# Weighted sums of an attention kernel on four column tiles of 32 channels by 128 rows, two tiles of keys at a time

## The chip, the cores and the metric

The kernel runs on one core of one Trainium2 chip. The metric is device time in microseconds (us), from the start of the program to its end, without the host. Two runs of the kernel before gave 1893.37 and 1893.46 us, a median of 1893.41. The profile is one execution of the same program taken by the hardware profiler.

The engines of a core work side by side and wait for one another by semaphores: PE (TensorE, matrix multiplication into PSUM), DVE (VectorE), ACT (ScalarE), POOL (GpSimd) and SP (SyncE, which only issues transfers). The profile shows PE's matmuls and its weight loads (PEld) apart.

## The reference

The input is a batch of 8 images of 64 channels and 64 x 64 pixels (4096 pixels per image). Layer 0 is attention over the pixels of an image, layer 1 three binarized convolutions with a gate. Cut to what matters:

```python
q, k, v = wq @ x + bq, wk @ x + bk, wv @ x + bv           # each 64 x 4096 per image
q, k = q - mean(q), k - mean(k)
sim = softmax(q.T @ k / 8, axis=keys)                      # 4096 x 4096 per image
out = sim @ v + out_unary                                  # out_unary: one vector per image
x = x + out
# layer 1: three convolutions (1x1, 3x3, 5x5) of sign(x) with sign weights, scaled and summed
s = conv1(sign(x)) + conv3(sign(x)) + conv5(sign(x))
result = s * sigmoid(gate(mean(s))) + x
```

## The kernel before, in words

**Tiles.** Two images make a pair; image 0 takes partitions 0 to 63, image 1 partitions 64 to 127 (one partition per channel). There are 4 pairs. The 4096 queries of a pair are cut into 8 blocks of 512 columns, so the whole kernel runs 32 blocks one after the other. Within a block, the 4096 keys of an image are cut into 32 tiles of 128 keys. All matrices of the attention are 32-bit floats.

**One step of a block** handles one tile of keys for both images:

- `scores` (L573): four matmuls of 64 rows (channels) by 64 columns (half of the keys, `h`), for two halves and two images `b`, over 512 queries. The result `ps`, 128 keys x 2 images x 512 queries, lies in two PSUM banks. The pool `ps_s` holds two such results, and other stages borrow from it.
- ACT takes the exponential (L595) of `ps` into `e` in SBUF. The pool `ep` holds five such tiles; the partial sums of the softmax of the block before (`e_parts`, L652) borrow one of the five from step 0 to step 7.
- `weighted` (L598): four matmuls (L607) of 64 rows (half of the keys) by 64 columns (channels of one image). Half `h` accumulates into bank `acc[h]`, over all 32 tiles of keys. So each bank has the sum over half of the keys, for both images.
- `summed` (L615): DVE adds `e` to `es` (L625; L623 for the first two), the sums of the softmax. Tiles 5, 11, 17 and 23 are added in DRAM instead, by a DMA of POOL's queue (L644, L646).

**The loop** (`attend`, L1217) keeps the weighted sum one tile behind: in each step it issues the scores of tile j, then the weighted sum and the adding of tile j - 1, then what the plan has put at this step. `pending` carries the tile that is still to be summed, also from one block to the next. On PE, scores and weighted sums so take turns.

**The plan** (`plan`, L1227) is a list of further work by step number. In step 0, after the last weighted sum of the block before: `weighted_out` (L627) copies `acc[0]` by ACT (L632) and `acc[1]` by DVE (L633) to SBUF; `send` and `gather` move the partial sums through DRAM; `mix_rows` (L1125) computes the queries of a coming block (`pq`, L563) and the convolution's row products of the block three back (L906, L996), for which it borrows one `ps_s` tile (`banks5`) and both `acc` banks. DVE and ACT read these products with L937, L939 and L944. Steps 5 to 7 fold the partial sums on DVE (`fold_first` L661, `fold` L666 and L667, `fold_last` L671). Step 13 adds the two halves of the weighted sum (`added`, L717), step 15 divides and adds the input (`finish`, L721 and L722), steps 16 to 20 take signs. In the last four blocks of a pair, steps 14 and 22 compute value tiles of the next pair (`values`, `pv` L414), which also borrow a `ps_s` tile; ACT copies them (L422) and takes an exponential (L429). Steps 18 to 24 prepare the convolution's row combinations on DVE. Four times in the run `unary_end` (`po`, L461) multiplies on the whole 128 x 128 array.

**The last block** cuts its queries into two parts (`PARTS`, L43): 384 columns with 32 steps, and 128 columns with 8 steps of four tiles of keys each. Its plan (`plan_last`, L1346) puts the work of the step by this number of steps, and adds two calls of `mix` (L1072) for the convolution, which borrow from `ps_s`.

The order on each engine follows the program's order of issue (`manual_schedule`), apart from what the recording layer interleaves between engines; a buffer's next user waits for its last user.

Of the kernel before, what the change touches and what calls it, by code (L numbers as in the profile page):

```python
# [18 lines left out]
F32 = mybir.dt.float32  # L19
# [3 lines left out]
ALU = mybir.AluOpType  # L23
# [3 lines left out]
P = 128  # L27
# [4 lines left out]
QB = 512  # L32
NQ = N // QB
NK = N // P
# [8 lines left out]
PARTS = ((slice(0, 384), 1), (slice(384, QB), 4))  # L43
# [4 lines left out]
def conv_seq_kernel(ctx, tc, x, wqv, wk, wv, w1, w3, w5, wtap, gw, out):  # L48
    nc = tc.nc
# [3 lines left out]
    img = [slice(0, C), slice(C, P)]  # L53
# [5 lines left out]
    fp = ctx.enter_context(tc.tile_pool(name="fp", bufs=1))  # L59
# [219 lines left out]
    class Pair:  # L279
# [3 lines left out]
        def __init__(self, name, xt):  # L283
            self.name, self.x = name, xt
            self.xs = sm.tile([P, 8], F32, tag="xs", name=f"xs_{name}")
            self.q, self.x2, self.s, self.y1, self.acc, self.o = {}, {}, {}, {}, {}, {}
            self.sides = []
            self.es, self.r, self.joint, self.sc, self.gap, self.t = {}, {}, None, None, None, None

# [308 lines left out]
        def weighted(self, qb, j, e, part=(slice(0, QB), 1)):  # L598
            cols, n = part
            w = cols.stop - cols.start  # L600
            if j == 0:
                self.acc[qb] = acc_banks(f"acc_{self.name}_{qb}_{cols.start}")
            for t in range(n * j, n * j + n):
                at = (t - n * j) * w
                for b in range(2):
                    for h in range(2):
                        nc.tensor.matmul(  # L607
                            self.acc[qb][h][img[b], 0:w],
                            self.v[img[h], t, img[b]],
                            e[img[h], b, at : at + w],  # L610
                            start=(t == 0),
                            stop=(t == NK - 1),
                        )

        def summed(self, qb, j, e, dram=False, begin=nc.vector):  # L615

# [10 lines left out]
        def weighted_out(self, qb, cols=slice(0, QB)):  # L627

            acc, w = self.acc.pop(qb), cols.stop - cols.start
            if cols.start == 0:  # L630
                self.o[qb] = [self.tile(fp, f"o{h}", qb) for h in range(2)]
            nc.scalar.copy(self.o[qb][0][:, cols], acc[0][:, 0:w])  # L632
            nc.vector.tensor_copy(self.o[qb][1][:, cols], acc[1][:, 0:w])  # L633

# [68 lines left out]
        def reciprocals_wide(self, qb, cols):  # L705
            if cols.start == 0:
                self.r[qb] = self.tile(fp, "r", qb)
            for a in range(cols.start, cols.stop, P):
                c = slice(a, min(a + P, cols.stop))
                sums, at = self.sums_p  # L710
                nc.vector.reciprocal(self.r[qb][:, c], sums[:, c.start - at : c.stop - at])

        def added(self, qb, cols=slice(0, QB)):
            if cols.start == 0:
                self.x2[qb] = self.tile(bp, "x2", qb)
            o = self.o[qb]
            nc.vector.tensor_tensor(self.x2[qb][:, cols], o[0][:, cols], o[1][:, cols], ALU.add)  # L717

        def finish(self, qb, cols=slice(0, QB)):
            x2 = self.x2[qb][:, cols]  # L720
# [486 lines left out]
    def acc_banks(name):  # L1207
        return [ps_a.tile([P, QB], F32, tag=f"acc{h}", name=f"{name}_{h}") for h in range(2)]

    def misc_banks(name):  # L1210
        return [m_tile(f"{name}_{h}") for h in range(2)]

# [2 lines left out]
        return slice(pr * P, (pr + 1) * P)  # L1215

    def attend(pairs, early):  # L1217
        pending = None
        n_blocks = n_pairs * NQ

        def block(g):
# [5 lines left out]
        def plan(g):  # L1227
# [4 lines left out]
            def put(i, f, *a):  # L1232
                at.setdefault(i, []).append((f, a))
# [36 lines left out]
            if g >= 1:  # L1270
                put(5, p.fold_first, b)
                put(6, p.fold, b)
                put(7, p.fold_last, b)
                put(8, p.spread, b)
                put(9, p.check_block, b, 0)
                put(11, p.check_block, b, 1)
                at0 = 13 if g < n_blocks - 1 else 11
                put(at0, p.added, b)
                put(at0 + 2, p.finish, b)
                put(at0 + (3 if g < n_blocks - 1 else 4), p.signs_wide, b, 2)  # L1280
                put(at0 + (5 if g < n_blocks - 1 else 6), p.signs_wide, b, 1)
                put(at0 + 7, p.signs, b)
# [63 lines left out]
        def plan_last():  # L1346

            at, (first, _) = {}, PARTS
            for i, steps in plan(n_blocks - 1).items():
                at[i * QB // first[0].stop] = steps  # L1350

            def put(i, f, *a):
                at.setdefault(i, []).append((f, a))

            p, b = pairs[-1], NQ - 1
            cols = first[0]
            r1 = cols.stop // HH
            put(NK - 5, lambda: mix(None, rows(n_blocks - 3), one_bank, score_banks))
            put(NK - 2, lambda: mix(None, (p, p.joint_rows(0, 6)), one_bank, score_banks))
            put(NK, p.weighted_out, b, cols)  # L1360
            put(NK + 1, p.added, b, cols)
            put(NK + 1, p.sums_wide, b, first)
            put(NK + 1, p.reciprocals_wide, b, cols)
            put(NK + 2, p.finish, b, cols)
            put(NK + 3, lambda: p.check(p.r[b][:, cols], n_blocks - 1))
            put(NK + 4, p.signs_wide, b, 2, 0, r1)
            put(NK + 5, p.signs_wide, b, 1, 0, r1)
            put(NK + 6, p.signs, b, 0, r1)
            return at

        for g in range(n_blocks):
            pr, qb = divmod(g, NQ)
            last = g == n_blocks - 1
            at = plan_last() if last else plan(g)
            p = pairs[pr]
            parts = PARTS if last else ((slice(0, QB), 1),)
            steps = [(part, j) for part in parts for j in range(NK // part[1])]
            for i, (part, j) in enumerate(steps):
                first = g == 0 and j < len(early)
                e = early[j] if first else p.scores(qb, j, None, part)  # L1380
                new = (p, (qb, j, e), part)
                if pending is not None:
                    pending[0].weighted(*pending[1], pending[2])

                    begin = nc.gpsimd if pending[2] == PARTS[1] else nc.vector
                    pending[0].summed(*pending[1], g < n_blocks - 1, begin)
                for f, a in at.pop(i, ()):
                    f(*a)
                pending = new
            assert not at, at.keys()  # L1390
        pending[0].weighted(*pending[1], pending[2])
        pending[0].summed(*pending[1])


        p, b = pairs[-1], NQ - 1
# [2 lines left out]
        r0, r1 = cols.start // HH, ROWS  # L1398
        p.weighted_out(b, cols)
        p.sums_wide(b, part)  # L1400
        p.added(b, cols)
        p.reciprocals_wide(b, cols)
        p.check(p.r[b][:, cols], n_pairs * (NQ + 1), (0,))
        p.finish(b, cols)
# [1 line left out]
            p.signs_wide(b, n, r0, r1, None)  # L1406
            p.copy_signs(b, n, r0, r1, (nc.vector.tensor_copy, nc.gpsimd.tensor_copy))
        p.signs(b, r0, r1, nc.gpsimd.tensor_copy)

        def acc_bank(h):  # L1410
            return lambda name: [ps_a.tile([P, QB], F32, tag=f"acc{h}", name=name)]

        def count(side):
            p.check(p.r[b][:, cols], n_pairs * (NQ + 1), (side,))
# [69 lines left out]
    with tc.If(n_good < P):  # L1484
        neg = fp.tile([P, QB], F32, tag="t5", name="neg")
        nc.vector.memset(neg, 0.0)
        with tc.For_i(0, n_pairs * P, P) as row:
# [12 lines left out]
            for qb in range(NQ):  # L1500
                mix((p, qb), None)
                for h in range(QB // P):
                    part = sm.tile([P, 2, NQ], F32, tag="part", name=f"part_{qb}_{h}")
                    for kb_ in range(NQ):
                        ps = ps_s.tile([P, 2, QB], F32, tag="s", name=f"px_{qb}_{h}_{kb_}")
                        for b in range(2):
                            nc.tensor.matmul(
                                ps[:, b, :],
                                p.q[qb][img[b], bass.ts(h, P)],
                                p.x[img[b], bass.ts(kb_, QB)],  # L1510
                                start=True,
                                stop=True,
                            )
                        nc.vector.tensor_reduce(part[:, :, kb_], ps, AX.X, ALU.max)
                    nm = sm.tile([P, 2], F32, tag="nmx", name=f"nmx_{qb}_{h}")
                    nc.vector.tensor_reduce(nm, part, AX.X, ALU.max, negate=True)
                    pn = m_tile(f"pn_{qb}_{h}")
                    for b in range(2):
                        nc.tensor.matmul(
                            pn[C * b : C * b + 1, 0:P], nm[:, b : b + 1], ident, start=True, stop=True  # L1520
                        )
                        nc.vector.tensor_copy(
                            neg[C * b : C * b + 1, bass.ts(h, P)], pn[C * b : C * b + 1, 0:P]
                        )
                for j in range(NK):
                    e = p.scores(qb, j, neg)
                    p.weighted(qb, j, e)
                    p.summed(qb, j, e)
                p.weighted_out(qb)
                p.sums_wide(qb)  # L1530
                p.reciprocals_wide(qb, slice(0, QB))
                p.added(qb)
                p.finish(qb)
            p.copy_tile()
            for qb in range(NQ):
# [66 lines left out]
```

## Time and profile before

| what | value |
|---|---|
| median of two runs | 1893.41 us |
| span of the profiled execution, first to last instruction | 1889.9 us |
| granted TensorE clock, mean | 0.999 of full speed |
| PE busy with matmuls | 1875.6 us (99%) |
| PE weight loads | 800.7 us (42%), beside matmuls |
| DVE busy | 1602.8 us (85%) |
| ACT busy | 1269.5 us (67%) |
| POOL busy | 131.2 us (7%) |
| DMA, mean over the span | 75 GB/s |

How to read it: a group of instructions is a line of the kernel, its engine and operation, the result and the inputs by the program's names, its shape and count, then busy time in us, mean ns of one instruction, and the time for which the engine stood idle just before it with what ended that. A shape such as `64*64 64x512` is the part of the array (rows * columns), then partitions x elements of the streamed operand. Matmuls are pipelined and their ends are modelled, so starts say more than ends. A matmul on 32-bit floats leaves two records. The chain that ended last is followed back from the last instruction, at each step to what released it.

### The profile page before, as it was taken

The page shows a single profiled execution, that of the slowest core. Times are in us where ns is not written, and L with a number is a line of the kernel's source. Part 1 is how long each engine was busy: PE and PEld are TensorE (multiplying, and loading weights), DVE is VectorE, ACT ScalarE, POOL GpSimd, SP SyncE. Part 2 cuts the span into 40 slices and gives each one's busy share as a digit, 9 for nine tenths or more (in the row PEclk, how much of TensorE's full clock was granted, in tenths as well). Part 3 has the DMA queues.
Part 4 walks back from the last instruction along what each step waited for, and adds up shares of the span by engine and source line. Part 5 has one row for each costly group of instructions (what it writes and reads, how often), then busy time and mean ns, then how long its engine had stood idle before and what let it go on. Part 6 is the DMA issues. An engine that isn't in the chain of part 4 may idle for free.

```text
span 1889.9 us, 51407 instructions
## 1 busy us (share of the span) xinstructions
PE 1875.6 (99%) x22016; PEld 800.7 (42%) x22016; DVE 1602.8 (85%) x2526; ACT 1269.5 (67%) x1630; POOL 131.2 (7%) x176
## 2 busy tenths in 40 slices
PE   9999999999999999999999999999999999999997
PEld 4345344443344434443434444434433344444345
DVE  7888888889888888888888888888888888888886
ACT  6666776666666676666666667666666666666664
POOL 0000000000000000000000000000000000000001
PEclk9999999999999999999999999999999999999999
DMA  4334333333333433333333444243333333333311
GB/s 125 65 65 103 78 67 71 67 58 72 68 70 89 117 82 81 65 73 66 58 72 68 97 111 89 58 83 66 72 67 58 71 78 90 86 71 65 82 36 53
DMA packets 73461, 142.50 MB, mean 75 GB/s; under 512 B 10444, under 2 KB 41480, under 8 KB 73096
## 3 DMA queue, kind: packets, MB, share of 16 engines
q0 software_dynamic: 22320, 81.27, 23.3%
q1 hardware_dynamic: 50328, 56.73, 10.3%
q8 instruction: 174, 2.85, 0.6%
q10 hardware_dynamic: 576, 1.13, 0.2%
q14 instruction: 63, 0.52, 0.1%
HBM read 39.27 MB, written 89.78 MB: 68 GB/s over the span
## 4 chain that ended last, share of the span: by engine, by line
PE 98%; DVE 1%; ACT 0%; DMA 0%; issue 0%; ACTq 0%; DVEq 0%
PE ps L582 46%; PE acc L607 46%; PE z L906 2%; PE pv L414 1%; PE z L996 1%; PE pq L563 1%; DMA es<-e 0%; PE z_5e L906 0%; ACT e L595 0%; PE warm L157 0%; DVE es L625 0%; DVE sb L1069 0%; PE pq L535 0%; PE su L696 0%; DVE es_j L1028 0%
## 5 line engine op out<-in xcount | busy, mean ns | idle before, releaser
L595 ACT ACTIVATE e<-ps 128x1024 f32<-128x1024 f32 (+1 forms) x1030 | 1048.4, 1018 | 568.2 <-PE ps L582 553.0
L625 DVE TENSOR_TENSOR es<-es,e 128x1024 f32<-128x1024 f32 (+1 forms) x842 | 1019.7, 1211 | 192.5 <-ACT e L595 178.2
L582 PE MATMUL ps<-q,x 64*64 64x512 f32 (+2 forms) x8448 | 1090.3, 577 | 1.5 <-DVE q L347 0.8
L607 PE MATMUL acc<-e,v 64*64 64x512 f32 (+2 forms) x8432 | 1085.8, 576 | 1.3 <-ACT e L595 1.3
L607 PEld LDWEIGHTS acc<-e,v 64*64 64x64 f32 x8432 | 335.0, 131 | 545.8 <-ACT e L595 314.8
L582 PEld LDWEIGHTS ps<-q,x 64*64 64x64 f32 x8448 | 359.5, 133 | 483.3 <-issue 262.3
L646 POOL DMA_DIRECT2D es<-e x93 | 80.1, 861 | 903.8 <-ACT e L595 598.7
L976 DVE SCALAR_TENSOR_TENSOR sb<-pt,sb 128x256 f32<-128x256 f32 x174 | 65.8, 418 | 0.0
L906 PEld LDWEIGHTS <-wc 64*64 64x64 bf16 x3364 | 58.8, 106 | 1.7 <-issue 0.8
L646 POOL DMA_DIRECT2D es<-es x31 | 26.6, 857 | 438.6 <-DVE es L625 438.6
L623 DVE TENSOR_TENSOR es<-e,e 128x1024 f32<-128x1024 f32 (+1 forms) x31 | 37.7, 1216 | 17.2 <-ACT e L595 17.2
L906 PE MATMUL z<-ec,wc 64*64 64x128 bf16 x1392 | 51.5, 217 | 0.0
L906 PE MATMUL z<-t,wc 64*64 64x128 bf16 x1392 | 51.1, 216 | 0.1
L754 ACT ACTIVATE s<-x,wqv_s 128x512 bf16<-128x512 f32 (+2 forms) x66 | 46.2, 702 | 0.2 <-DVE x L722 0.2
L939 ACT ACTIVATE pt<-z,frac 128x256 f32<-128x256 f32 (+1 forms) x58 | 30.6, 578 | 16.8 <-PE z L906 16.8
L644 POOL DMA_DIRECT2D es<-e x31 | 17.5, 563 | 334.5 <-ACT e L595 323.3
L633 DVE COPY o<-acc 128x512 f32<-128x512 f32 (+2 forms) x33 | 22.3, 675 | 9.4 <-PE acc L607 9.3
L950 DVE TENSOR_TENSOR pt<-pt 128x384 f32<-128x384 f32 x58 | 29.6, 552 | 0.0
L414 PEld LDWEIGHTS pv<-wx,x 64*64 64x64 f32 x992 | 21.5, 134 | 16.1 <-issue 8.6
L661 DVE TENSOR_TENSOR e_parts<-e_parts 128x512 f32<-128x512 f32 x31 | 21.3, 686 | 6.1 <-DMA e_parts<-es 6.0
L722 DVE SCALAR_TENSOR_TENSOR x<-x,ou,x 128x512 f32<-128x512 f32 (+2 forms) x33 | 24.3, 736 | 1.2
L422 ACT COPY v<-pv 128x512 f32<-128x512 f32 x31 | 18.2, 587 | 8.4 <-PE pv L414 8.4
(201 smaller groups left out, 893.9 us busy)
## 6 DMA issues: line engine op xcount, KB each, us to landing
es<-e POOLq DMA_DIRECT2D x124, 512.0 KB, 5.1
es<-es POOLq DMA_DIRECT2D x31, 512.0 KB, 5.3
e_parts<-es SPq DMA_DIRECT2D x124, 128.0 KB, 3.0
r<-rc SPq DMA_DIRECT2D x62, 128.0 KB, 2.8
out<-sb SPq DMA_DIRECT2D x27, 256.0 KB, 2.9
x<-in_x SPq DMA_DIRECT2D x24, 256.0 KB, 4.3
ec<-t SPq DMA_DIRECT2D x29, 99.0 KB, 4.5
xc<-in_x SPq DMA_DIRECT2D x30, 72.0 KB
```

Of the source, the lines that this page charges most:

```text
L414: nc.tensor.matmul(pv[img[h], b, i * w : (i + 1) * w], self.x[img[b], bass.ds((4 * g + i) * P + h * H, H)], self.wx[img[b], 0:w], start=Tr ...
L582: nc.tensor.matmul(ps[img[h], b, i * w : (i + 1) * w], self.x[img[b], bass.ds((n * j + i) * P + h * H, H)], self.q[qb][img[b], cols], star ...
L595: nc.scalar.activation(e, ps[:, :, 0 : n * w], AF.Exp, scale=1.0 / 8.0)
L607: nc.tensor.matmul(self.acc[qb][h][img[b], 0:w], self.v[img[h], t, img[b]], e[img[h], b, at : at + w], start=(t == 0), stop=(t == NK - 1),)
L623: begin.tensor_tensor(self.es[qb], self.first, e, ALU.add)
L625: nc.vector.tensor_tensor(self.es[qb], self.es[qb], e, ALU.add)
L646: nc.gpsimd.dma_start(out=out, in_=e, accum_op=ALU.add)
L754: nc.scalar.activation(sy[n][0][:, rows, pad : pad + HH], self.x2[qb][:, r0 * HH : r1 * HH].rearrange("p (h w) -> p h w", w=HH), AF.Sign, ...
L906: nc.tensor.matmul(z[img[b], :].rearrange("p (q w) -> p q w", w=HH), wc[k][img[h], n, c * C : c * C + C], src[:, first : first + step + 1 ...
L939: nc.scalar.activation(out, z, AF.Identity, scale=frac[:, by : by + 1])
L950: nc.vector.tensor_tensor(self.pairs[:, :, :, r, :], t[:, 0:3, 0], t[:, 0:3, 1], op)
L976: nc.vector.scalar_tensor_tensor(out, x, by, out, ALU.mult, ALU.add, **gap)
```

## The change

1. `weighted` now issues four matmuls with all 128 rows (all keys of the tile) and 32 columns (half of the channels of one image) each; group `g` takes image `g // 2`. All four write one bank, each its own 32 partitions. One accumulator holds the whole sum.
2. With one accumulator, `weighted_out` is one ACT copy straight into `x2`; the DVE copy and the later addition (`added`) go, with all calls.
3. The loop takes two steps at a time: the scores of tiles i and i + 1, then the weighted sums and addings of the two tiles before, then what the plan has at steps i and i + 1.

```diff
@@ weighted
-                self.acc[qb] = acc_banks(f"acc_{self.name}_{qb}_{cols.start}")
+                self.acc[qb] = acc_bank(0)(f"acc_{self.name}_{qb}_{cols.start}")[0]
             for t in range(n * j, n * j + n):
                 at = (t - n * j) * w
-                for b in range(2):
-                    for h in range(2):
-                        nc.tensor.matmul(
-                            self.acc[qb][h][img[b], 0:w],
-                            self.v[img[h], t, img[b]],
-                            e[img[h], b, at : at + w],
-                            start=(t == 0),
-                            stop=(t == NK - 1),
-                        )
+                for g in range(4):
+                    nc.tensor.matmul(
+                        self.acc[qb][32 * g : 32 * g + 32, 0:w],
+                        self.v[:, t, 32 * g : 32 * g + 32],
+                        e[:, g // 2, at : at + w],
+                        start=(t == 0),
+                        stop=(t == NK - 1),
+                    )
@@ weighted_out
             if cols.start == 0:
-                self.o[qb] = [self.tile(fp, f"o{h}", qb) for h in range(2)]
-            nc.scalar.copy(self.o[qb][0][:, cols], acc[0][:, 0:w])
-            nc.vector.tensor_copy(self.o[qb][1][:, cols], acc[1][:, 0:w])
+                self.x2[qb] = self.tile(bp, "x2", qb)
+            nc.scalar.copy(self.x2[qb][:, cols], acc[:, 0:w])
@@ added: removed, with its calls in the plans, at the end and in the fallback path
-        def added(self, qb, cols=slice(0, QB)):
-            if cols.start == 0:
-                self.x2[qb] = self.tile(bp, "x2", qb)
-            o = self.o[qb]
-            nc.vector.tensor_tensor(self.x2[qb][:, cols], o[0][:, cols], o[1][:, cols], ALU.add)
@@ moved up, from the end of attend
+    def acc_bank(h):
+        return lambda name: [ps_a.tile([P, QB], F32, tag=f"acc{h}", name=name)]
@@ attend
-        pending = None
+        pending = []
...
-            for i, (part, j) in enumerate(steps):
-                first = g == 0 and j < len(early)
-                e = early[j] if first else p.scores(qb, j, None, part)
-                new = (p, (qb, j, e), part)
-                if pending is not None:
-                    pending[0].weighted(*pending[1], pending[2])
-
-                    begin = nc.gpsimd if pending[2] == PARTS[1] else nc.vector
-                    pending[0].summed(*pending[1], g < n_blocks - 1, begin)
-                for f, a in at.pop(i, ()):
-                    f(*a)
+            for i in range(0, len(steps), 2):
+                new = []
+                for part, j in steps[i : i + 2]:
+                    first = g == 0 and j < len(early)
+                    e = early[j] if first else p.scores(qb, j, None, part)
+                    new.append((p, (qb, j, e), part))
+                for old in pending:
+                    old[0].weighted(*old[1], old[2])
+                    begin = nc.gpsimd if old[2] == PARTS[1] else nc.vector
+                    old[0].summed(*old[1], g < n_blocks - 1, begin)
+                for k in (i, i + 1):
+                    for f, a in at.pop(k, ()):
+                        f(*a)
                 pending = new
             assert not at, at.keys()
-        pending[0].weighted(*pending[1], pending[2])
-        pending[0].summed(*pending[1])
+        for old in pending:
+            old[0].weighted(*old[1], old[2])
+            old[0].summed(*old[1])
```

More of the change, by code (lines that the diff above doesn't have):

```diff
@@ L285, in __init__ @@
             self.xs = sm.tile([P, 8], F32, tag="xs", name=f"xs_{name}")
-            self.q, self.x2, self.s, self.y1, self.acc, self.o = {}, {}, {}, {}, {}, {}
+            self.q, self.x2, self.s, self.y1, self.acc = {}, {}, {}, {}, {}
             self.sides = []
@@ L1277, in plan @@
                 at0 = 13 if g < n_blocks - 1 else 11
-                put(at0, p.added, b)
                 put(at0 + 2, p.finish, b)
@@ L1360, in plan_last @@
             put(NK, p.weighted_out, b, cols)
-            put(NK + 1, p.added, b, cols)
             put(NK + 1, p.sums_wide, b, first)
@@ L1400, in attend @@
         p.sums_wide(b, part)
-        p.added(b, cols)
         p.reciprocals_wide(b, cols)
@@ L1408, in attend @@
         p.signs(b, r0, r1, nc.gpsimd.tensor_copy)
-        def acc_bank(h):
-            return lambda name: [ps_a.tile([P, QB], F32, tag=f"acc{h}", name=name)]
         def count(side):
@@ L1531, in conv_seq_kernel @@
                 p.reciprocals_wide(qb, slice(0, QB))
-                p.added(qb)
                 p.finish(qb)
```

## The prediction

> **What bounds the kernel now.** I read the shares of the engines first, then the chain that ended last, then the costliest groups.
>
> ```profile
> PE 1875.6 (99%) x22016; PEld 800.7 (42%) x22016; DVE 1602.8 (85%) x2526; ACT 1269.5 (67%) x1630; POOL 131.2 (7%) x176
> ...
> PE 98%; DVE 1%; ACT 0%; DMA 0%; issue 0%; ACTq 0%; DVEq 0%
> PE ps L582 46%; PE acc L607 46%; PE z L906 2%; PE pv L414 1%; PE z L996 1%; PE pq L563 1%; DMA es<-e 0%; PE z_5e L906 0%; ACT e L595 0%; PE warm L157 0%; DVE es L625 0%; DVE sb L1069 0%; PE pq L535 0%; PE su L696 0%; DVE es_j L1028 0%
> ...
> L595 ACT ACTIVATE e<-ps 128x1024 f32<-128x1024 f32 (+1 forms) x1030 | 1048.4, 1018 | 568.2 <-PE ps L582 553.0
> L582 PE MATMUL ps<-q,x 64*64 64x512 f32 (+2 forms) x8448 | 1090.3, 577 | 1.5 <-DVE q L347 0.8
> L607 PE MATMUL acc<-e,v 64*64 64x512 f32 (+2 forms) x8432 | 1085.8, 576 | 1.3 <-ACT e L595 1.3
> ```
>
> TensorE is 98% of the chain, and scores (L582) and weighted sums (L607) idle 1.5 and 1.3 us in all. Whatever lengthens TensorE lengthens the kernel. The timeline of TensorE in a steady stretch gives its beat:
>
> ```profile
> 1003.33 1.06 PE L607 MATMUL acc<-e,v 64*64 64x512 f32 x8
> 1004.19 1.06 PE L582 MATMUL ps<-q,x 64*64 64x512 f32 x8
> 1005.05 1.06 PE L607 MATMUL acc<-e,v 64*64 64x512 f32 x8
> ```
>
> A group starts every 0.86 us: four matmuls, two records each, so two passes of 0.43 us in which four 64x64 tiles stream together. Of the 1.06, 0.43 is the first pass and 0.59 one record (L607's mean by shape is 589 ns); the remaining 0.04 is the stagger of the four starts.
>
> **How the array changes shape.** Only `po` (L461), on 128x128, stands between such groups, four times. The timeline around the last of them, matmuls, then weight loads:
>
> ```profile
> 1404.88 1.06 PE L607 MATMUL acc<-e,v 64*64 64x512 f32 x8
> 1405.87 0.49 PE L461 MATMUL po<-vu,ones 128*128 128x130 f32 x2
> 1406.29 1.09 PE L582 MATMUL ps<-q,x 64*64 64x512 f32 x8
> 1407.20 0.61 PE L607 MATMUL acc<-e,v 64*64 64x512 f32 x4
> ```
> ```profile
> 1404.88 0.17 PEld L607 LDWEIGHTS acc<-e,v 64*64 64x64 f32 x4
> 1405.87 0.30 PEld L461 LDWEIGHTS po<-vu,ones 128*128 128x128 f32 x2 [0.81 <-DVE pt L944]
> 1406.29 0.21 PEld L582 LDWEIGHTS ps<-q,x 64*64 64x64 f32 x8
> ```
>
> The load for `po` begins 0.99 us after the group, not 0.86: 0.13 late, of which 0.04 is the stagger, 0.09 an empty array. The following scores take 0.91 instead of 0.86: their weights couldn't be loaded ahead, 0.05. After a switch the stagger is 0.02 (the next groups last 1.04).
>
> **The Trainium skill.** *TensorEngine Tiling (Array Packing)*, Key Properties, says that changing the tiling mode, not just the tile, drains TensorE; the 0.09 agrees. *TensorE: Matmul & The Clock Gate*, LDWEIGHTS, gives columns/1.2 ns: 53 for 64 columns, as the trace has, 27 for 32. The same page, "What overlaps and what doesn't", has loads overlap matmuls only where row groups differ, which would spoil tiles of 128 rows. The trace disagrees: the sums at the end, two column tiles of 128 rows,
>
> ```profile
> 1869.69 1.09 PE L696 MATMUL su<-es,ones 128*64 128x128 f32 x16 [0.15 <-DVE es L625]
> ```
>
> take 1.09 - 0.27 (a record) = 0.82 us for 16 passes of 128 columns, which one after the other would be 16 x 0.107 (a quarter of 0.43) = 1.7. Two ran together, loads hidden.
>
> **The change, part by part.**
>
> (a) *Weighted sums.* Before: 64 rows x 64 columns, four at once. After: 128 rows x 32 columns, four at once, the same number of instructions and columns. Streaming stays at 0.86 us per key tile if four such tiles stream together: gain zero. No row shows four; two of 128 rows do (L696), and the skill's packing table (that page, Part 3) has three column tiles at 2.38x. I take 0.86; the far bound, two at a time, is a rival. Below 0.86 I see no way: the pass of 0.107 us for 128 columns in 128-row tiles is the same rate as 0.43 for 512.
>
> (b) *Switches.* Scores stay 64x64, so each pair of key tiles switches twice. Into the sums: 0.02 stagger + 0.09 drain + 0.03 load = 0.14. Back: 0.02 + 0.09 + 0.05 = 0.16. Together 0.30 per pair. Pairs: 31 blocks x 16 + 20 in the last (32 + 8 tiles) = 516. 516 x 0.30 = **+155 us**, all on the path, since nothing else runs on TensorE in the gap. Bounds: 0.27 with the load into the sums hidden (139), 0.38 if its four loads queue up, 4 x 0.027 (196).
>
> (c) *Order of scores.* A score tile has two buffers. Row products of the convolution (L906) borrow one of them in step 0. Before, one weighted sum lay between the borrowing and the tile that needs it back; the timeline:
>
> ```profile
> 999.04 1.06 PE L582 MATMUL ps<-q,x 64*64 64x512 f32 x8
> 999.33 0.48 DVE L944 SCALAR_TENSOR_TENSOR pt<-z_5e,frac,pt 128x256 f32<-128x256 f32 x1 [0.31 <-PE z_5e L906]
> 999.81 0.75 DVE L944 SCALAR_TENSOR_TENSOR pt<-z,frac,pt 128x512 f32<-128x512 f32 x1
> 999.90 1.06 PE L607 MATMUL acc<-e,v 64*64 64x512 f32 x8
> 1000.61 0.32 PEld L582 LDWEIGHTS ps<-q,x 64*64 64x64 f32 x8 [0.54 <-DVE pt L944]
> ```
>
> L944 frees the buffer at 1000.56, the loads follow at 1000.61, and the sum of 999.90 covers it. After, scores 2 and 3 follow the row products at once: score 3 would start at 999.90 and gets its weights at 1000.61 + 0.05. Stall 0.76 us, in the 29 blocks that have L944: **+22 us**. Behind it on TensorE wait the sums 0 and 1 and everything later; exp of tile 3 is late too, ending near 1002.8, some 1.5 us before score 5 wants its buffer. Bounds: 0.3 (were the long L944 the first: 0.48 earlier) to 1.1 (another DVE step of 0.36 ahead): 8 to 32.
> The value tiles `pv` (L414) borrow a buffer in the same way: ACT's copy (586 ns) and exp (183 ns) end 0.91 us after the last `pv`, about when the second score wants it: 0.07 x 31 = +2. The two late `mix` calls: +2.
>
> (d) *Removed: one copy and the addition.* L633 (33 x 0.68) and L717 (33 x 0.68) go, some 44 us of DVE. TensorE's stream hides them (DVE is 1% of the chain): gain 0. Were DVE the bound, it would be up to 44. ACT's copy stays, 580 ns; the row products that reuse its bank start later now, by the switch.
>
> (e) *Exponentials and their five buffers.* Before, an exp had 0.4 us in hand (the one of the scores at 999.04 starts at 1000.17, lasts 1.02, and its sum starts at 1001.61); now a whole pair. But four tiles are alive instead of two, and one buffer is lent to the partial sums until step 7. In the built order exp 7 waits for L671 of DVE. Adding up DVE's rows from 1000.56 (three sums of 1.22, L950 1.02, L964 0.49, L976 0.76, L661 0.69, one more sum, L666 0.43, L667 0.45, L671 0.41: 9.1) puts L671's end at 1009.7; exp 7 could begin near 1009.3 and now ends near 1010.8, a microsecond before score 9 wants its buffer (pairs of 3.74 from score 2 at 999.04 and the stall put it near 1011.8). No cost; bounds 0 to 0.06 us per pair, 30 us. The DMA of tiles 5, 11, 17, 23 (5.1 us) has over 8 us before its buffer returns. No DMA or queue moves otherwise.
>
> Sum: 155 + 22 + 2 + 2 = 181. The profiled execution spans 1889.9; the median 1893.4 lies 3.5 above, which is outside first and last instruction and stays. 1893.4 + 181 = **2074 us**, 9.6% slower. Bounds together: 139 + 8 = 147 to 196 + 32 + 4 + 30 = 262, so 2040 to 2155.
>
> **Rivals.**
> 1. *The buffers bind:* DVE reaches L671 and the sums late, and exps wait block by block; 0.15 to 0.2 us more per pair, 77 to 103: about 2165. For: one buffer is spare. Against: the walk above, and DVE falls from 85% to some 75%.
> 2. *Column tiles stream only two at a time:* each sum takes 1.72, 1024 x 0.86 = +880: 2950. For: each array row must take four streams of e, where now it takes two. Against: the skill's table.
> 3. *Not slower: no drain.* The gaps around `po` were its own semaphore waits (the load names DVE L944), and switches between matmuls that wait for nothing are free. Then only (c) remains: 1893 + 26 = 1919, within 2%. It decides below 38/516 = 0.02 us a pair after (c)'s 26. Against: all four `po` show 0.81 idle before the load, one with "issue" as releaser.
> 4. *Sums stream faster:* to win 2% each must fall below 0.86 by 0.04 and (b) must vanish: some 1850. Nothing shows it.
>
> **Chances and range.** Forecast 0.77, rivals 0.09, 0.05, 0.06, 0.03. About 2% is what can be told from no change. Faster 0.03, same 0.06, slower 0.91. The range takes the bounds and most of rival 1: 2040 to 2175.
>
> **What would show it.** Right: L606 rows `128*32`; four starts close together, groups 0.86 apart inside a mode; gaps of 0.14 to 0.16 at each change; TensorE waiting on the successor of L944 in 29 blocks. Wrong: passes of sums 0.86 apart (rival 2), gaps of nothing (3), exp waits on DVE with TensorE idle (1).

## The result and the profile after

The changed kernel takes 2064.7 us, median of two runs (2064.64 to 2064.76), against 1893.41 us: a ratio of 1.0904, with a 95% interval of 1.0873 to 1.0936. It is slower by 171.3 us. The forecast was 2074, the range 2040 to 2175. The profiled executions span 2062.9 us after and 1889.9 before, 173.0 us more.

The page of the kernel after, in the order of the lines shown of before (its line numbers are those of the changed file: L606 is the weighted sum, L936 the former L944):

```profile
span 2062.9 us, 51266 instructions
...
PE 2034.0 (99%) x22016; PEld 585.6 (28%) x22016; DVE 1580.9 (77%) x2460; ACT 1225.3 (59%) x1630; POOL 131.3 (6%) x176
...
PE 98%; DVE 2%; issue 0%; ACT 0%; DVEq 0%
PE acc L606 46%; PE ps L582 46%; PE z L898 2%; DVE pt L936 1%; PE pv L414 1%; PE pq L563 1%; PE z L988 1%; PE z_5e L898 0%; PE warm L157 0%; DVE sb L1061 0%; PE pq L535 0%; PE po L461 0%; PE su L694 0%; DVE es_j L1020 0%; DVE sb L1020 0%
...
L595 ACT ACTIVATE e<-ps 128x1024 f32<-128x1024 f32 (+1 forms) x1030 | 998.6, 1016 | 716.7 <-PE ps L582 557.2
L582 PE MATMUL ps<-q,x 64*64 64x512 f32 (+2 forms) x8448 | 1007.3, 588 | 14.5 <-DVE pt L936 12.1
L606 PE MATMUL acc<-e,v 128*32 128x512 f32 (+2 forms) x8432 | 983.8, 585 | 0.0
```

TensorE is busy for 99% as before, with as many instructions, and still 98% of the chain. Its busy time even reads lower for each of the two groups (983.8 after 1085.8): records of 0.59 us cover the gaps at the switches, and where groups followed every 0.86 us before, their records overlapped and that time counted for both. So busy time doesn't show the loss. The starts do. The timeline of TensorE in a steady stretch of the kernel after (start, duration, both in us):

```profile
1098.98 1.95 PE L582 MATMUL ps<-q,x 64*64 64x512 f32 x16
1100.86 1.92 PE L606 MATMUL acc<-e,v 128*32 128x512 f32 x16
1102.71 1.95 PE L582 MATMUL ps<-q,x 64*64 64x512 f32 x16
1104.59 1.92 PE L606 MATMUL acc<-e,v 128*32 128x512 f32 x16
```

Two groups of scores take 1.88 us and two weighted sums 1.85; a pair of key tiles 3.73 where before it took 4 x 0.859 = 3.44. The weight loads of the same stretch, with ACT's exponentials and the last fold of the partial sums on DVE (L669, the former L671):

```profile
1099.89 0.15 PEld L582 LDWEIGHTS ps<-q,x 64*64 64x64 f32 x4 [0.28 <-issue]
1100.14 1.94 ACT L595 ACTIVATE e<-ps 128x1024 f32<-128x1024 f32 x2 [1.73 <-PE ps L582]
1100.52 0.42 DVE L669 TENSOR_REDUCE rec<-e_parts 128x8 f32<-128x256 f32 x1
1100.86 0.16 PEld L606 LDWEIGHTS acc<-e,v 128*32 128x32 f32 x8 [0.81 <-issue]
1101.32 0.13 PEld L606 LDWEIGHTS acc<-e,v 128*32 128x32 f32 x4 [0.30 <-issue]
1101.74 0.13 PEld L606 LDWEIGHTS acc<-e,v 128*32 128x32 f32 x4 [0.30 <-issue]
1102.71 0.21 PEld L582 LDWEIGHTS ps<-q,x 64*64 64x64 f32 x8 [0.84 <-ACT e L595]
```

Inside a shape, loads run ahead, one set in each pass of 0.43 us (1101.32, 1101.74). At a change of shape the first set comes only when the array is empty, with its matmul (1100.86), and the second set right behind. Before the sums the loads wait for nothing that the profile names ("issue"). Before the scores they name ACT (1102.71), but its two exponentials had ended by 1100.14 + 1.94 = 1102.08, 0.63 us earlier. So neither gap is a semaphore's.

The start of a block, after the row products of the convolution:

```profile
1090.82 1.04 PE L582 MATMUL ps<-q,x 64*64 64x512 f32 x8
1091.57 0.75 DVE L936 SCALAR_TENSOR_TENSOR pt<-z,frac,pt 128x512 f32<-128x512 f32 x1
1092.38 0.21 PEld L582 LDWEIGHTS ps<-q,x 64*64 64x64 f32 x8 [1.40 <-DVE pt L936]
1092.38 1.09 PE L582 MATMUL ps<-q,x 64*64 64x512 f32 x8 [0.52 <-DVE pt L936]
```

Scores 3 would start at 1090.82 + 0.86 = 1091.68. They get their weights at 1092.38, 0.06 us after L936 has ended, and need 0.05 to load them: 0.75 us lost.

### The profile page after: what moved, and what is told of

The parts are those of the page before. It is cut to its first block, busy times and chain, and to the rows that moved or that the text cites. A ratio compares the mean times of both kernels' runs of the same rounds, so it can differ in the third digit from the quotient of the medians.

```text
span 2062.9 us, 51266 instructions
## 1 busy us (share of the span) xinstructions
PE 2034.0 (99%) x22016; PEld 585.6 (28%) x22016; DVE 1580.9 (77%) x2460; ACT 1225.3 (59%) x1630; POOL 131.3 (6%) x176
## 4 chain that ended last, share of the span: by engine, by line
PE 98%; DVE 2%; issue 0%; ACT 0%; DVEq 0%
PE acc L606 46%; PE ps L582 46%; PE z L898 2%; DVE pt L936 1%; PE pv L414 1%; PE pq L563 1%; PE z L988 1%; PE z_5e L898 0%; PE warm L157 0%; DVE sb L1061 0%; PE pq L535 0%; PE po L461 0%; PE su L694 0%; DVE es_j L1020 0%; DVE sb L1020 0%
## 5 line engine op out<-in xcount | busy, mean ns | idle before, releaser
L595 ACT ACTIVATE e<-ps 128x1024 f32<-128x1024 f32 (+1 forms) x1030 | 998.6, 1016 | 716.7 <-PE ps L582 557.2
L582 PE MATMUL ps<-q,x 64*64 64x512 f32 (+2 forms) x8448 | 1007.3, 588 | 14.5 <-DVE pt L936 12.1
L606 PE MATMUL acc<-e,v 128*32 128x512 f32 (+2 forms) x8432 | 983.8, 585 | 0.0
L582 PEld LDWEIGHTS ps<-q,x 64*64 64x64 f32 x8448 | 271.0, 132 | 679.8 <-ACT e L595 249.4
L606 PEld LDWEIGHTS acc<-e,v 128*32 128x32 f32 x8432 | 220.0, 109 | 713.9 <-issue 693.0
L570 DVE TENSOR_SCALAR q<-pq,mx 128x224 f32<-128x224 f32 x30 | 13.5, 450 | 101.0 <-PE pq L563 101.0
L631 ACT COPY x<-acc 128x512 f32<-128x512 f32 (+2 forms) x33 | 18.9, 573 | 26.7 <-PE acc L606 26.7
L929 DVE TENSOR_SCALAR pt<-z,frac 128x256 f32<-128x256 f32 x29 | 14.0, 483 | 20.4 <-PE z L898 20.4
L436 DVE TENSOR_TENSOR cl<-v,eu 128x512 f32<-128x512 f32 x32 | 22.1, 690 | 7.4 <-ACT eu L429 7.4
```

The lines of the kernel that those rows point to most:

```text
L436: nc.vector.tensor_tensor(tv, self.v[:, 4 * g : 4 * g + 4, :].rearrange("p t (b c) -> p b t c", b=2), self.eu[:, :, 4 * g : 4 * g + 4].uns ...
L582: nc.tensor.matmul(ps[img[h], b, i * w : (i + 1) * w], self.x[img[b], bass.ds((n * j + i) * P + h * H, H)], self.q[qb][img[b], cols], star ...
L595: nc.scalar.activation(e, ps[:, :, 0 : n * w], AF.Exp, scale=1.0 / 8.0)
L606: nc.tensor.matmul(self.acc[qb][32 * g : 32 * g + 32, 0:w], self.v[:, t, 32 * g : 32 * g + 32], e[:, g // 2, at : at + w], start=(t == 0), ...
```

## Experiments

The kernel before, measured beside them, took 1891.6 to 1892.0 us.

**The paired loop alone.** The kernel before, with the loop of the changed one; the sums stay on 64x64 tiles, with two accumulators, the copy and the addition.

```diff
-            for i, (part, j) in enumerate(steps):
+            for i in range(0, len(steps), 2):
...
+                for part, j in steps[i : i + 2]:   # both scores, then both sums
```

> The kernel before with the paired loop alone: weighted sums stay 64 rows by 64 columns, so nothing switches shape. Theory (the switch costs 0.30 us a pair, the borrowed score buffer 0.70 us in 29 blocks): only the buffer remains, 1893 + 29 x 0.70 + 31 x 0.10 for the value tiles = 1916 us, or a few us less, since the small losses in the stream of before (some 5 us) may go. Rival (the paired order itself starves TensorE of exponentials and buffers): the most of the 171 us comes here too, over 2000 us.

Measured: 1926.7 us (1925.9 to 1927.3), ratio 1.0184 (1.0167 to 1.0201). The paired order costs 35 us, a fifth of what the change costs, and 11 us more than the theory gave it. The two waits that count, from the waits of its trace, TensorE's and ACT's:

```profile
PE ps L582 <- DVE pt L944: 12.2, 23, 0.7
PE ps L582 <- ACT e L595: 4.0, 8, 1.2
...
ACT e L595 <- DVE rec L671: 81.8, 27, 4.1
```

The first is the borrowed score buffer (the idle time shown is a part of the 0.75, the record of the matmul before covers the rest). The last is new: exponentials wait for L671, the last reader of the partial sums' buffer, and through them the scores of tile 8. One such place in the timeline:

```profile
317.83 1.90 PE L607 MATMUL acc<-e,v 64*64 64x512 f32 x16
318.20 0.42 DVE L671 TENSOR_REDUCE rec<-e_parts 128x8 f32<-128x256 f32 x1
318.70 1.94 ACT L595 ACTIVATE e<-ps 128x1024 f32<-128x1024 f32 x2 [2.91 <-DVE rec L671]
319.78 0.21 PEld L582 LDWEIGHTS ps<-q,x 64*64 64x64 f32 x8 [0.93 <-ACT e L595]
```

The two sums take 319.78 - 317.83 = 1.95 us where 1.72 would do, and the two scores behind them another 0.11 too long. By the starts, TensorE loses 13.6 us there over 29 blocks, 0.33 us in most of them and up to 1.6. The value tiles' borrowing costs more than the 0.10 put in: the two scores behind `pv` take 1.87 us instead of 1.72, 0.16 us, 31 times.

**One tile at a time.** The changed sums with the loop of before, so that the shape changes twice a tile.

```diff
-            for i in range(0, len(steps), 2):
+            for i, (part, j) in enumerate(steps):   # scores j, then the sum of j - 1
```

> The changed weighted sums, but the loop of before, one tile of keys at a time: the array changes shape twice a tile instead of twice a pair. Theory: 1032 x 0.30 = 310 us of switches, no wait for the borrowed buffer: 1893 + 310 - 5 = 2198 us. Rival (four streams of 128 rows are slower in themselves, whatever stands next to them): as much as in the changed kernel without the buffer's 20, about 2045 us. Rival (a switch costs nothing where nothing waits): near 1893 us.

Measured: 2190.9 us (2190.6 to 2192.1), ratio 1.1582 (1.1563 to 1.1601). TensorE's timeline:

```profile
1099.97 1.09 PE L582 MATMUL ps<-q,x 64*64 64x512 f32 x8
1100.99 1.06 PE L606 MATMUL acc<-e,v 128*32 128x512 f32 x8
1101.99 1.09 PE L582 MATMUL ps<-q,x 64*64 64x512 f32 x8
```

Scores take 1.02 us and a sum 1.00, where 0.859 each would do without a switch: 0.16 and 0.14 more, as in the changed kernel. The loss goes with the number of switches: (2190.9 - 1891.9) / 2064 = 0.145 us each. Four streams of 128 rows cost nothing by themselves, and the rival that switches are free is out.

**Two column tiles of 64.**

```diff
-                for g in range(4):
+                for b in range(2):
                     nc.tensor.matmul(
-                        self.acc[qb][32 * g : 32 * g + 32, 0:w],
-                        self.v[:, t, 32 * g : 32 * g + 32],
-                        e[:, g // 2, at : at + w],
+                        self.acc[qb][img[b], 0:w],
+                        self.v[:, t, img[b]],
+                        e[:, b, at : at + w],
```

> The changed kernel with two column tiles of 64 channels by 128 rows in place of four of 32: half of the instructions, the same columns streamed. Theory: two tiles at once do the same work in the same time, and each switch into the sums loads 64 columns (0.053 us) instead of 32 (0.027): 2064.7 + 516 x 0.026 = 2078 us. If four streams had been slower than two, this would be faster than the changed kernel by what they cost.

Measured: 2072.0 us (2071.8 to 2072.4), ratio 1.0951 (1.0933 to 1.0970); its span is 7.7 us longer than the changed kernel's.

```profile
1099.42 1.95 PE L582 MATMUL ps<-q,x 64*64 64x512 f32 x16
1101.30 1.94 PE L606 MATMUL acc<-e,v 128*64 128x512 f32 x8
1103.17 1.95 PE L582 MATMUL ps<-q,x 64*64 64x512 f32 x16
```

The sums take 1.87 instead of 1.85. Here the rows alone change (64 columns in both), and the array empties all the same. The wider load costs 0.026, but two starts are 0.007 us apart where four spread over 0.020, which gives half of it back; the expectation had left that out. The direction, not the intervals (they overlap), carries this.

**Rows kept, columns changed.** On top of the paired loop alone:

```diff
-                for b in range(2):
+                for g in range(4):
                     for h in range(2):
                         nc.tensor.matmul(
-                            self.acc[qb][h][img[b], 0:w],
-                            self.v[img[h], t, img[b]],
-                            e[img[h], b, at : at + w],
+                            self.acc[qb][h][32 * g : 32 * g + 32, 0:w],
+                            self.v[img[h], t, 32 * g : 32 * g + 32],
+                            e[img[h], g // 2, at : at + w],
```

> The paired loop with weighted sums of 64 rows by 32 columns, eight tiles in two banks, with the copy and the addition of before: the rows of a tile are those of the scores, only the columns change. If any change of the tile's shape empties the array: 516 x 0.30 on top of the paired loop, 1914 + 155 = 2069 us. If only a change of the rows does: as the paired loop alone, about 1914 us. If twice as many instructions can't be issued in time: above 2100.

Measured: 2083.7 us (2083.1 to 2083.9), ratio 1.1012 (1.0994 to 1.1031): 157 us above the paired loop alone, near the 155 of the first case (the base was put 13 too low).

```profile
1100.09 1.95 PE L607 MATMUL acc<-e,v 64*32 64x512 f32 x32
1101.96 1.95 PE L582 MATMUL ps<-q,x 64*64 64x512 f32 x16
1103.84 0.66 PE L607 MATMUL acc<-e,v 64*32 64x512 f32 x8
```

A group takes 1.87 or 1.88 us. That 157 meets 155 is in part luck. By the starts a pair takes 1.88 + 1.88 - 2 x 1.72 = 0.32 us longer, 165 us in all, because the starts of eight tiles spread over 0.047 us. In return the 13.6 us that the paired loop loses at L671 are gone. A change of the columns alone empties the array as well; and eight tiles with twice the instructions still stream at full rate.

**The pair at step 2 taken one by one**, in the changed kernel:

```diff
                     new.append((p, (qb, j, e), part))
+                    if g >= 3 and i == 2 and len(new) == 1:
+                        old = pending.pop(0)
+                        old[0].weighted(*old[1], old[2])
+                        old[0].summed(*old[1], g < n_blocks - 1)
```

> The changed kernel, but in the 29 blocks with row products the pair of steps 2 and 3 is taken one by one: scores 2, sum 0, scores 3, sum 1. Theory (scores 3 wait 0.70 us for the borrowed buffer, no other): the wait is covered by sum 0, two switches more cost 0.30, net -0.40 x 29 = -12: 2053 us. If the 0.70 us is not the buffer's but DVE's lateness in general: the two switches come on top, 2064.7 + 9 = 2074 us.

Measured: 2056.7 us (2056.0 to 2057.3), ratio 1.0871 (1.0852 to 1.0891); the span is 7.6 us shorter than the changed kernel's. TensorE's waits:

```profile
PE pm L314 <- DVE pt L936: 2.0, 3, 0.7
PE po L461 <- DVE pt L936: 2.0, 3, 0.7
PE ps L582 <- DVE sb L1020: 1.1, 1, 1.1
```

The scores' wait for L936 is gone from the 23 blocks that had it. In six others a small matmul (`pm` or `po`) stands ahead of scores 2 and waits for the same instruction; there the wait stays, while the two switches were paid in all 29. 29 x 0.30 - 23 x 0.75 = -8.6, against 7.6 measured in the span and 8.0 in the medians. So the 0.75 us is the buffer's.

**Without the copy and the addition**, in the kernel before:

```diff
-            nc.vector.tensor_copy(self.o[qb][1][:, cols], acc[1][:, 0:w])
...
-            nc.vector.tensor_tensor(self.x2[qb][:, cols], o[0][:, cols], o[1][:, cols], ALU.add)
```

> The kernel before without the DVE copy of the second accumulator and without the addition: the weighted sums of half of the keys are left out of the result, all matmuls stay. Theory (44 us of DVE lie beside TensorE's stream): 1893 us, within 2 us. If DVE set the pace anywhere: up to 44 us less.

Measured: 1891.96 us beside 1891.63, ratio 1.0000 (0.9991 to 1.0009). Its page has DVE at 1565.6 us busy instead of 1602.8. That work was hidden whole.

**The two waits of the paired loop.** First the same step-2 edit as above, now on 64x64 tiles, where it adds no switch:

> The paired loop on 64x64 tiles of the first experiment (1926.7 us), with the pair of steps 2 and 3 taken one by one in the 29 blocks with row products. Nothing switches here. Theory: the wait for the borrowed score buffer, 0.75 us a block in that kernel's trace, is covered: 1926.7 - 22 = 1905 us. If the wait moves on to another buffer instead: near 1926 us.

Measured: 1926.1 us (1925.0 to 1927.0), ratio 1.0178 (1.0161 to 1.0195): nothing gained. The buffer's wait is gone and another has taken its whole place; TensorE's waits and ACT's:

```profile
PE ps L582 <- ACT e L595: 22.2, 29, 1.5
...
ACT e L595 <- DVE rec L671: 100.0, 28, 4.3
```

L671 ends when DVE gets to it. TensorE, earlier by 0.75 us, waits for it that much longer. Then the folding earlier, with the pairs left as they are:

```diff
-                put(5, p.fold_first, b)
-                put(6, p.fold, b)
-                put(7, p.fold_last, b)
+                put(4, p.fold_first, b)
+                put(4, p.fold, b)
+                put(5, p.fold_last, b)
```

> The paired loop on 64x64 tiles of the first experiment (1926.7 us), with the folding of the partial sums put at steps 4, 4 and 5 in place of 5, 6 and 7. Theory (its exponentials of tiles 6 and 7 wait for L671, and scores 8 for them, 0.22 us in the 27 blocks where the trace names L671): about 1926.7 - 6 = 1921 us. If DVE then waits for the DMA of the partial sums instead: 1927 us or more.

Measured: 1914.8 us (1914.4 to 1915.8), ratio 1.0121 (1.0105 to 1.0138): 12 us, most of the 13.6 that TensorE lost, not the 6 that I had read from the common gap alone. Then both edits:

> Both edits of the last two experiments on the paired loop with 64x64 tiles: the pair of steps 2 and 3 one by one, and the folding at steps 4, 4 and 5. Theory (two waits in a row in each block, for the borrowed score buffer and then for L671; either edit alone leaves the later one): from the 1914.8 us of early folding the 17 us of the buffer's wait in its trace go too, 1898 us. If the early folding left L671 so late that it takes the place of the buffer once more: near 1915 us.

Measured: 1901.6 us (1900.3 to 1902.7), ratio 1.0053 (1.0036 to 1.0069). Together they give 25 us, the first alone 0.6: two waits in a row, of which the later decides. What stays, 10 us, has in it the value tiles' borrowing (0.16 us, 31 times, 5 us) and the six blocks with a small matmul (4.5 us, an estimate from the 0.75 us of the others); no run splits it.

No version beat the kernel before: its stream has next to no gap to give.

## Why the prediction was right, point by point

- *(a) Streaming.* Right. Four column tiles of 128 rows stream together: passes 0.43 us apart, starts 0.02 spread. The rival of two at a time is out, and so is a faster sum.
- *(b) Switches.* Right in mechanism and size. Averaged over steady stretches a pair takes 3.732 us after and 3.434 before: 0.30 us, 154 us over 516 pairs. The experiment with twice the switches gives 0.145 each.
- *(c) Score buffer.* Right: 0.75 us where 0.76 was forecast, 22 us. The value tiles were put too low: 0.16 us instead of 0.07 (5 us instead of 2). The two scores behind `pv` take 1.98 us, where the 1.72 of streaming and 0.11 for stagger and empty array would give 1.83. Of the 2 us for the late `mix` calls about 1 came: TensorE's waits for what reads their products (L1028, L1020 after) are 1.7 us in all, before 0.6.
- *(d) Copy and addition.* Right: nothing.
- *(e) Exponentials.* Right for this kernel, and by less than it looked. The wait of exp 7 for L671 that I added up is real, but it belongs to the other kernel: it costs 13.6 us in the paired loop on 64x64 tiles. In the changed kernel four exponentials wait for it, 1.6 us in all, and TensorE loses nothing; in the block shown L669, its new number, ends 8.6 us after L936 (1092.32 to 1100.94), where 9.1 was added up. What covers it is the beat, slower by the switches, and not the copy and the addition that left DVE: the kernel with sums of 64x32 keeps both, switches as well, and loses nothing there either. My walk used the beat of 3.74 us, but didn't say that the term rests on it. Rival 1's mechanism exists, in a kernel without switches.

The sum was 181; the spans differ by 173.0. With the sizes measured the terms are 154 + 22 + 5 + 1 = 182. About 7 less comes from a term that the sum lacked: small losses in the stream of before that the changed kernel doesn't have. They are 46 gaps of 0.05 us (31 of them behind value tiles), 1.6 us in the matmuls of the value tiles, gaps of 1.01, 0.86 and 0.36, and some of 0.15 to 0.25. The rest, some 2 us, I can't place. The value tiles were priced too low and this term was left out, with opposite signs; both are small beside the 154.

The 3.5 us between the median of before and the span of the profile were misread. In every run whose time and span are both on record, the time is 1.7 to 1.9 us above its own span. The rest of the 3.5 is therefore a difference between executions: the two that gave 1893.41 took longer than the profiled one, and longer than the medians of 1891.6 to 1892.0 measured later. The forecast of 2074 started from 1893.4 and so carries these 1.7 us; against the later medians the change costs some 173 us rather than 171.3.

## What to carry to other kernels

Two kinds of matmul that take turns should have the same tile shape: here each change of shape, of rows, columns or both, cost 0.14 to 0.16 us, and grouping two of a kind halves the number of changes at the price of buffers that come back later. Look at starts, not at busy time: both kernels are 99% busy. A wait that you remove may only uncover the next one, and a slower engine may hide it; remove both before you judge either.

## What the runs showed of the hardware

- A change of the tile's shape costs the stagger of the last starts (0.007 us for each tile after the first), 0.09 us of empty array, and the load of the first weights: 0.05 us for 64 columns, 0.03 for 32. The runs show it between 64x64 and 128x32, 128x64 and 64x32; into 128x128 (`po`) the array stood empty for the same 0.09 us, after a stagger of 0.04.
- 32-bit matmuls on four tiles of 128x32 or eight of 64x32 streamed at the rate of four 64x64 tiles, 0.43 us for a pass of 512 columns, and their later weight loads were hidden, although all four column tiles use the same rows.
